# A four-layer graph network on one Trainium2 core: the list schedule gets other durations, a charge for TensorE's changes of mode, and a shorter period

## The chip, the cores and the metric

The kernel runs on one core of a Trainium2 chip. The core has five engines with instruction queues of their own: TensorE (PE in the profile, its weight loads PEld), VectorE (DVE), ScalarE (ACT), GpSimd (POOL) and SyncE (SP, which here issues DMAs only). Each engine takes its instructions in the order in which the program gives them. The metric is device time in microseconds for one launch; several runs are taken and their median is given. A profile is one further execution.

## The reference

The input x is 32 samples of 512 nodes by 256 features, in float32, and one adjacency matrix of 512 x 512 for all samples. Four layers follow each other, each with a layer norm and a ReLU ahead of it and an addition to x behind it:

```python
h = max(layernorm(x), 0); x = x + L0(h)   # 4 heads of 64: softmax(q k^T / 8, masked) v, then wo
h = max(layernorm(x), 0); x = x + L1(h)   # MLP 256->512, GAT without mask, MLP 512->256, GAT with mask
h = max(layernorm(x), 0); x = x + L2(h)   # GAT, 4 heads of 64, masked
h = max(layernorm(x), 0); x = x + L3(h)   # GAT, 8 heads of 32, masked, with a prior, then W_out
# a GAT's weights: softmax over j of leaky_relu(f1[i] + f2[j])
```

Samples are independent of each other; within a sample the layers are not.

## The kernel before, in words

After the weights and masks are prepared, `pipelined` (L493) builds the program of all 32 samples as a list of steps, and a planner puts the steps in order.

**What a step is.** `q = Plan(nc, PERIOD)` (L525) stands in for the engines. A call such as `q.vector.tensor_tensor(...)` is only recorded (`Plan.add`, L87): it becomes a `Step` with its engine, its duration from `cost` (L253), the tiles that it touches, and the earlier steps that it must follow. A step of TensorE inside `with q.unit(t):` joins several matmuls to one step of t microseconds, which are then issued together. All recorded calls are issued from L217, so that the profile has this one line for nearly everything and groups are told apart by the names of tiles.

**How the order comes about.** `Plan.order` (L116) simulates the engines. Each step has a tail, the longest chain of durations behind it in its sample, with `HOP` for each handover between steps, and a due time (L129), where `PERIOD` is 90:

```python
step.due = s * self.period - step.tail
```

Steps that take something out of a PSUM bank on another engine than TensorE get a due time 1000 earlier. Then, over and over, of all steps whose predecessors are planned and for which buffers are to be had, the one with the smallest pair (start, due) is taken (L113, L167 to L182); its start is the later of the time when its engine is free and the time when its inputs are ready. The clock of the engine goes on by the step's duration (L186). So due times decide between steps that could start at the same time, and start decides before due. At most `AHEAD` = 3 samples beyond the oldest unfinished one may take part (L171). Buffers are counted: 61 blocks of 128 x 512 in SBUF, 8 PSUM banks, 4 tiles x. The result is one order; each engine's queue is filled in that order (`issue`, L213), and on the chip semaphores hold an instruction until its inputs are there. The planner's durations don't slow anything on the chip; they only set the order.

**The work of a sample.** `norm_t` (L546): `bn_stats` and `bn_aggr` on VectorE, `rs` as a power on GpSimd, `h` on VectorE, transposes into `pt` on TensorE, and `hT` on ScalarE. Matrix products over 128 x 128 of weights are `feature_major`, `node_major`, `node_major2` and `weighted` (tiles `mm` and `av`); they and the transposes use the whole array of TensorE. Three kinds of units use a part of it at a time:

- `sc` in layer 0 (L651): two heads at once, each on 64 rows of the array. ScalarE then takes the exponential, and VectorE multiplies the mask in.
- Layer 0's `av` and `sm` (L658): four products of 64 columns, two at a time, and four sums of 32 columns at once. `f1p` of layer 1 (L683): four products of 32 columns at once.
- Layers 2 and 3, `separable` (L803): for one block of 128 keys, j, VectorE makes four tiles `p` (L837), and a unit (L841) multiplies them into `av` and `sm`, with 64 and 32 columns in layer 2 (duration 2.85) and 32 columns in layer 3 (duration 1.92). `R`, which `p` reads, comes over DRAM by DMA (`rd`).

`normalise` (L604) takes sums through DRAM, for a reciprocal on all partitions, with four to seven DMAs on SP.

Of the kernel before, what the change touches and what calls it, by code (L numbers as in the profile page):

```python
# [19 lines left out]
N = 512  # L20
# [16 lines left out]
SAFE_PRIOR = 20.0  # L37


PERIOD = 90.0  # L40
BLOCKS, KEEP = 61, 12
KEEP_BANKS = 0

# [1 line left out]
class Step:  # L45


    def __init__(self, engine, busy):
        self.engine, self.busy, self.calls = engine, busy, []
        self.touches, self.before, self.after = [], [], []  # L50


class Plan:
# [6 lines left out]


    ENGINES = dict(tensor="PE", vector="DVE", scalar="ACT", gpsimd="POOL", sync="SP")
    HOP, AHEAD = 0.12, 3

    def __init__(self, nc, period):
        self.nc, self.period = nc, period
# [13 lines left out]
        self.samples.append([])  # L80
        self.history = {}

    def unit(self, busy):

        return _Unit(self, busy)

    def add(self, attribute, engine, op, args, kw):  # L87
        steps = self.samples[-1]
# [27 lines left out]
    def order(self):  # L116

        owners, left = {}, {}
        for s, steps in enumerate(self.samples):
            for step in steps:  # L120
                step.sample = s
                step.waits = len(step.before)
                step.ready = 0.0
                for name in step.touches:
                    left[name] = left.get(name, 0) + 1
                    owners[name] = s
            for step in reversed(steps):
                step.tail = step.lasts + max((n.tail + self.HOP for n in step.after), default=0.0)
                step.due = s * self.period - step.tail  # L129

                if step.engine != "PE" and any(self.tile_tag[name] == "bank" for name in step.touches):
                    step.due -= 1000.0
        free = {tag: [0.0] * bufs for tag, (bufs, _) in self.tags.items()}
        held = {}
        to_come = [{} for _ in self.samples]
        for name, s in owners.items():
            tag = self.tile_tag[name]
            to_come[s][tag] = to_come[s].get(tag, 0) + 1
        live, at = set(), {e: 0.0 for e in self.ENGINES.values()}
        open_ = {e: [] for e in at}  # L140
        for steps in self.samples:
            for step in steps:
                if not step.waits:
                    open_[step.engine].append(step)
        result, count = [], sum(map(len, self.samples))
        oldest = 0

        def slots(step):

            when, taken = 0.0, {}  # L150
            for name in step.touches:
                if name in live:
                    continue
                tag = self.tile_tag[name]
                keep = self.tags[tag][1]
                reserve = 0
                for s in range(oldest, step.sample):
                    if to_come[s].get(tag, 0):
                        reserve += max(0, min(keep, to_come[s][tag] + held.get((s, tag), 0)) - held.get((s, tag), 0))
                n = taken.get(tag, 0)  # L160
                if len(free[tag]) - n <= reserve:
                    return None
                when = max(when, sorted(free[tag])[n])
                taken[tag] = n + 1
            return when

        while len(result) < count:  # L167
            best = None
            for engine, waiting in open_.items():
                for step in waiting:  # L170
                    if step.sample > oldest + self.AHEAD:  # L171
                        continue
                    start = max(at[engine], step.ready)
                    if best is not None and self.key(start, step) >= best[0]:
                        continue
                    when = slots(step)
                    if when is None:
                        continue
                    start = max(start, when)
                    if best is None or self.key(start, step) < best[0]:  # L180
                        best = self.key(start, step), start, step
            assert best is not None, "the buffers do not suffice"  # L182
            _, start, step = best
            step.start = start
            open_[step.engine].remove(step)
            at[step.engine] = start + step.busy  # L186
            end = start + step.lasts
            for name in step.touches:
                tag, s = self.tile_tag[name], step.sample
                if name not in live:  # L190
                    live.add(name)
                    free[tag].remove(min(free[tag]))
                    held[s, tag] = held.get((s, tag), 0) + 1
                    to_come[s][tag] -= 1
                left[name] -= 1
                if not left[name]:
                    live.discard(name)
                    held[s, tag] -= 1
                    free[tag].append(end + self.HOP)
            for n in step.after:  # L200
                n.waits -= 1
                n.ready = max(n.ready, start + step.busy if n.engine == step.engine == "PE" else end + self.HOP)
                if not n.waits:
                    open_[n.engine].append(n)
            result.append(step)
            while oldest < len(self.samples) and not any(to_come[oldest].values()) and not any(
                n for (s, _), n in held.items() if s == oldest
            ):
                oldest += 1
        self.makespan = max(at.values())  # L210
        return result
# [15 lines left out]


class _Unit:
    def __init__(self, plan, busy):  # L230
        self.plan, self.busy = plan, busy

    def __enter__(self):
        self.plan.joined = Step("PE", self.busy)

    def __exit__(self, *_):
        self.plan.joined = None
# [14 lines left out]

def cost(engine, op, args, kw, out):  # L253

    n = 1
    for _, k in out.ap[1:]:
        n *= k
    if engine == "PE":
        if op == "transpose":
            return 0.11, 0.2  # L260
        return max(0.22, n * 0.00168), 0.2
    if engine == "ACT":
        return 0.08 + 0.00093 * n, 0.09 + (0.19 if "accum_out" in kw else 0.0)
    if engine == "DVE":
        if op == "reciprocal":
            return 0.07 + 0.00625 * n, 0.09
        return 0.066 + 0.00105 * n + (0.06 if op == "scalar_tensor_tensor" and n == N else 0.0), 0.09
    if engine == "POOL":
        return (1.05 if n < 16 else 0.2 + 0.0015 * n), 0.1
    return 0.1, 3.5  # L270


# [1 line left out]
def gnn_stack_kernel(ctx: ExitStack, tc: tile.TileContext, a: dict, out: bass.AP):  # L274
# [99 lines left out]
    with tc.tile_pool(name="prep", bufs=2) as prep, tc.tile_pool(name="prep_psum", bufs=1, space=PSUM) as pp:  # L374
# [17 lines left out]
        src = a["L2_a"]  # L392
# [60 lines left out]
        rows = []  # L453
# [39 lines left out]
    def pipelined(stack):  # L493
# [31 lines left out]
        q = Plan(nc, PERIOD)  # L525
# [103 lines left out]
        def layer0(xt):  # L629
# [15 lines left out]
            for m in range(KD):  # L645
                av, sm = bank("av"), bank("sm")
                for jj in range(0, NT, 2):
                    p = {}
                    for j in (jj, jj + 1):
                        sc = [bank("sc"), bank("sc")]  # L650
                        with q.unit(0.96):  # L651
                            for s, r in enumerate(rows):
                                q.tensor.matmul(sc[s], kT[m][r, col(j)], qT[m][r, :], start=True, stop=True)
                        for s in range(2):
                            p[j, s] = b = block("p0")
                            q.scalar.activation(b, sc[s], AF.Exp)
                            q.vector.tensor_tensor(b, b, mask0T[:, j, :], op=ALU.mult)
                    with q.unit(2.75):  # L658
                        for j in (jj, jj + 1):
                            for s, r in enumerate(rows):  # L660
                                q.tensor.matmul(
                                    av[r, :], half(v, j)[:, m * P + s * 64 : m * P + s * 64 + 64], p[j, s],
                                    start=(j == 0), stop=(j == NT - 1),
                                )

                        for n, b in enumerate(p.values()):
                            q.tensor.matmul(
                                sm[n * 32 : n * 32 + 32, :], ones[:, :32], b, start=(jj == 0), stop=(jj == NT - 2)
                            )
                normalise(oT[m], av, sm, 2, 2)  # L670
# [5 lines left out]
        def first_gat(o1):  # L676
# [3 lines left out]

            part, sd = block("part"), small("sd", NT, 2)
            f1p = bank("f1p")
            with q.unit(1.0):  # L683
                for k in range(KH):
                    q.tensor.matmul(f1p[k * 32 : k * 32 + 32, :], fr1a[:, k, :], o1[k], start=True, stop=True)
            q.scalar.copy(part, f1p)
# [116 lines left out]
        def separable(xt, w, nh, mask, bars):  # L803
# [23 lines left out]
            for g in range(nh // 4):  # L827
# [5 lines left out]
                for j in range(NT):  # L833
# [4 lines left out]
                            p[s], R[s], e[:, j, nh + h : nh + h + 1], mask[:, j, :], op0=ALU.max, op1=ALU.mult  # L838
                        )
                    st = dict(start=(j == 0), stop=(j == NT - 1))  # L840
                    with q.unit(1.92 if per == 4 else 2.85):  # L841
                        for s in range(4):
                            h, r0 = 4 * g + s, s % per * f
                            q.tensor.matmul(avs[s // per][r0 : r0 + f, :], half(v, j)[:, h * f : (h + 1) * f], p[s], **st)
# [464 lines left out]
```

## Time and profile before

| | |
|---|---|
| median of 3 runs | 4729.1 us (4728.43 to 4732.22) |
| the profiled execution | 4727.03 us |
| its span, first to last instruction | 4725.2 us |
| instructions | 55,985 |
| TensorE busy, matmuls | 4491.1 us (95%) |
| VectorE, ScalarE, GpSimd busy | 3061.7, 1642.7, 611.8 us |
| first matmul of the samples, last store issued | 108.2 us, 4721.3 us |

Busy time is the time that an engine's instructions cover. A matmul's record is longer than the distance to the next one's start, since they are pipelined, and its end is modelled. A chain line such as "2062.11 1.00 PE av L217 x8" has a start, a length and a number of instructions of one group in the sequence that ended last. A line of a wait names the waiting group and the one whose result it waited for, then the time in total, the number of times and the longest.

### The profile page before, as it was taken

How to read it: one execution, taken by the hardware profiler on the slowest of the kernel's cores; microseconds unless marked ns; L12 is line 12 of the kernel's file. 1: busy time of each engine (PE TensorE's matmuls, PEld its weight loads, DVE VectorE, ACT ScalarE, POOL GpSimd, SP SyncE). 2: the span in 40 equal slices, each digit the busy share in tenths (PEclk: the TensorE clock that was granted, in tenths of full speed). 3: DMA queues.
4: the chain of work that ended last, by engine and by line, in shares of the span. 5: the costliest groups of instructions: out<-in, count | busy, mean ns of one | idle time of the engine just before them, and what ended most of it. 6: DMA issues, size and time to landing. Idle time of an engine off the chain costs nothing.

```text
span 4725.2 us, 55985 instructions
## 1 busy us (share of the span) xinstructions
PE 4491.1 (95%) x20146; PEld 2069.3 (44%) x20146; DVE 3061.7 (65%) x6772; ACT 1642.7 (35%) x3508; POOL 611.8 (13%) x648
## 2 busy tenths in 40 slices
PE   2999999999999999999999999999999999999986
PEld 1444444444444444444444444444444444444442
DVE  5357676665667665677657776567666675667664
ACT  1343333333333333333333333333333333333321
POOL 1011111011101111111011110111110111101110
PEclk9999999999999999999999999999999999999997
DMA  2001111101111111111111111111011111111111
GB/s 85 10 18 50 34 46 38 43 30 37 38 40 35 44 39 30 46 44 37 35 36 34 44 46 37 33 38 49 28 44 31 41 42 45 29 39 35 42 36 42
DMA packets 168209, 183.04 MB, mean 39 GB/s; under 512 B 64370, under 2 KB 99956, under 8 KB 167924
## 3 DMA queue, kind: packets, MB, share of 16 engines
q1 hardware_dynamic: 161972, 173.10, 12.1%
q10 hardware_dynamic: 5408, 4.20, 0.3%
q8 instruction: 161, 2.64, 0.2%
q0 software_dynamic: 544, 2.10, 0.1%
q14 instruction: 124, 1.02, 0.1%
HBM read 159.92 MB, written 19.40 MB: 38 GB/s over the span
## 4 chain that ended last, share of the span: by engine, by line
PE 82%; DVE 10%; POOL 2%; ACT 2%; DMA 2%; issue 1%; SPq 0%; POOLq 0%; DVEq 0%; ACTq 0%
PE mm L217 34%; PE av L217 26%; PE sm L217 10%; PE pt L217 6%; PE sc L217 4%; DVE stats L217 2%; DVE x L217 2%; POOL rs L217 1%; DVE p L217 1%; DVE h L217 1%; PE f1p L217 1%; POOL p L217 1%; DVE ue L217 1%; DVE yT L217 1%; ACT e L217 1%
## 5 line engine op out<-in xcount | busy, mean ns | idle before, releaser
L217 PE MATMUL av<-p,v 128*128 128x512 f32 (+1 forms) x2048 | 726.2, 603 | 0.1
L217 DVE SCALAR_TENSOR_TENSOR p<-R,e,mask3T 128x512 f32<-128x512 f32 x1024 | 690.8, 748 | 14.3 <-DMA R<-rd 13.9
L217 PE MATMUL av<-p,vs 128*32 128x512 f32 (+1 forms) x3072 | 555.8, 604 | 14.1 <-DVE p L217 13.4
L217 PE MATMUL mm<-W_fc,o 128*128 128x512 f32 x1024 | 484.7, 602 | 0.0
L217 POOL TENSOR_TENSOR rs<-ve,mhalf 128x4 f32<-128x4 f32 x128 | 172.6, 1351 | 2087.1 <-DVE ve L217 1654.7
L217 PE MATMUL sm<-p,w 128*32 128x512 f32 x3072 | 424.8, 597 | 0.0
L217 DVE TENSOR_TENSOR p<-p,mask0T 128x512 f32<-128x512 f32 x512 | 348.1, 717 | 103.6 <-ACT p L217 102.6
L217 DVE SCALAR_TENSOR_TENSOR p<-R,e,mask1T 128x512 f32<-128x512 f32 x512 | 346.6, 748 | 80.1 <-DMA R<-rd 79.8
L217 ACT ACTIVATE p<-sc 128x512 f32<-128x512 f32 x512 | 274.8, 601 | 349.5 <-PE sc L217 348.0
L217 PEld LDWEIGHTS av<-p,v 128*128 128x128 f32 (+1 forms) x2048 | 243.4, 163 | 319.1 <-issue 274.4
L217 PEld LDWEIGHTS av<-p,vs 128*32 128x32 f32 (+1 forms) x3072 | 125.0, 118 | 369.8 <-issue 207.2
L217 POOL TENSOR_SCALAR p<-p,r 128x512 f32<-128x512 f32 x128 | 140.8, 1110 | 1103.2 <-DVE r L217 736.5
L217 PE MATMUL sc<-qT,kT 64*128 64x512 f32 x1024 | 280.9, 634 | 1.1 <-ACT s L217 0.9
L217 PEld LDWEIGHTS mm<-W_fc,o 128*128 128x128 f32 x1024 | 179.9, 190 | 183.1 <-issue 173.6
L217 PE MATMUL mm<-w,hT 128*128 128x272 f32 (+1 forms) x1024 | 255.8, 396 | 2.2 <-ACT hT L217 1.5
L217 DVE TENSOR_SCALAR h<-x,mv,rs 128x256 f32<-128x256 f32 x512 | 215.8, 475 | 62.0 <-POOL rs L217 61.6
L217 PE MATMUL mm<-o,mlp_w 128*128 128x512 f32 x512 | 235.0, 600 | 8.7 <-DVE o L217 8.7
L217 PE MATMUL pt<-ident,h 128*128 128x128 f32 x1024 | 169.4, 291 | 75.2 <-DVE h L217 73.3
L217 ACT COPY v<-mm 128x512 f32<-128x512 f32 (+1 forms) x256 | 122.7, 479 | 332.9 <-PE mm L217 325.8
L217 PE MATMUL mm<-hT,mlp_w 128*128 128x512 f32 x512 | 237.0, 605 | 0.8 <-ACT hT L217 0.7
L217 PE MATMUL av<-pT,v 128*128 128x512 f32 x512 | 233.3, 594 | 2.1 <-ACT pT L217 2.1
L217 DVE TENSOR_TENSOR vs<-mm,w 128x256 f32<-128x256 f32 x256 | 105.2, 420 | 188.6 <-ACT w L217 185.0
(188 smaller groups left out, 6124.5 us busy)
## 6 DMA issues: line engine op xcount, KB each, us to landing
R<-rd SPq DMA_DIRECT2D x384, 256.0 KB
x<-in_x_dram SPq DMA_DIRECT2D x32, 512.0 KB
rc<-s SPq DMA_DIRECT2D x128, 128.0 KB
rc<-s SPq DMA_DIRECT2D x256, 64.0 KB
out_dram<-x SPq DMA_DIRECT2D x32, 512.0 KB
adj<-in_adj_dram POOLq DMA_DIRECT2D x2, 1024.0 KB, 7.1
s<-sums SPq DMA_DIRECT2D x128, 8.0 KB
few<-s SPq DMA_DIRECT2D x128, 8.0 KB
```

Of the source, the lines that this page charges most:

```text
L217: getattr(getattr(self.nc, attribute), op)(*args, **kw)
```

## The change

It touches the planner and its numbers, and no computation.

- `PERIOD` is 55 for 90, and `HOP` 0.05 for 0.12.
- A step has a mode. Steps of TensorE are "full" unless a unit says otherwise: "rows" for `sc`, "columns" for the other units. When the planner compares steps of TensorE, one of another mode than the last planned one starts no earlier than `SWITCH` of that last mode after the engine is free.
- `cost` has other figures for most operations. For `bn_stats` and `reduce_max` it counts the elements of the input and no longer those of the output.
- The units have shorter durations. A unit covers one block of keys in `separable` as before.

```diff
-PERIOD = 90.0
+PERIOD = 55.0
@@ class Step
-    def __init__(self, engine, busy):
-        self.engine, self.busy, self.calls = engine, busy, []
+    def __init__(self, engine, busy, mode="full"):
+        self.engine, self.busy, self.mode, self.calls = engine, busy, mode, []
@@ class Plan
-    HOP, AHEAD = 0.12, 3
+    HOP, AHEAD = 0.05, 3
+    SWITCH = dict(full=0.094, columns=0.12, rows=0.2)
@@ Plan.order
-        result, count = [], sum(map(len, self.samples))
+        result, count, mode = [], sum(map(len, self.samples)), "full"
...
                     start = max(at[engine], step.ready)
+                    if engine == "PE" and step.mode != mode:
+                        start = max(start, at[engine] + self.SWITCH[mode])
...
             at[step.engine] = start + step.busy
+            if step.engine == "PE":
+                mode = step.mode
@@ class _Unit
-        self.plan, self.busy = plan, busy
+        self.plan, self.step = plan, Step("PE", busy, mode)
     def __enter__(self):
-        self.plan.joined = Step("PE", self.busy)
+        self.plan.joined = self.step
@@ def cost
+    src = args[1] if op in ("bn_stats", "reduce_max") else out
     n = 1
-    for _, k in out.ap[1:]:
+    for _, k in src.ap[1:]:
         n *= k
     if engine == "PE":
         if op == "transpose":
-            return 0.11, 0.2
-        return max(0.22, n * 0.00168), 0.2
+            return 0.109, 0.165
+        return max(0.2, n * 0.001676), 0.165
     if engine == "ACT":
-        return 0.08 + 0.00093 * n, 0.09 + (0.19 if "accum_out" in kw else 0.0)
+        return 0.08 + 0.00095 * n, 0.085 + (0.19 if "accum_out" in kw else 0.0)
     if engine == "DVE":
         if op == "reciprocal":
-            return 0.07 + 0.00625 * n, 0.09
-        return 0.066 + 0.00105 * n + (0.06 if op == "scalar_tensor_tensor" and n == N else 0.0), 0.09
+            return 0.07 + 0.00625 * n, 0.085
+        return 0.066 + 0.00105 * n + (0.06 if op == "scalar_tensor_tensor" and n == N else 0.0), 0.085
     if engine == "POOL":
-        return (1.05 if n < 16 else 0.2 + 0.0015 * n), 0.1
+        return (1.3 if n < 16 else 0.15 + 0.0016 * n), 0.1
@@ units
-                        with q.unit(0.96):
+                        with q.unit("rows", 0.86):
-                    with q.unit(2.75):
+                    with q.unit("columns", 2.63):
-            with q.unit(1.0):
+            with q.unit("columns", 0.86):
-                    with q.unit(1.92 if per == 4 else 2.85):
+                    with q.unit("columns", 1.72 if per == 4 else 2.6):
```

More of the change, by code (lines that the diff above doesn't have):

```diff
@@ L81, in begin, with unit @@
         self.history = {}
-    def unit(self, busy):
-        return _Unit(self, busy)
+    def unit(self, mode, busy):
+        return _Unit(self, mode, busy)
     def add(self, attribute, engine, op, args, kw):
@@ L229, with __init__ @@
 class _Unit:
-    def __init__(self, plan, busy):
-        self.plan, self.busy = plan, busy
+    def __init__(self, plan, mode, busy):
+        self.plan, self.step = plan, Step("PE", busy, mode)
     def __enter__(self):
-        self.plan.joined = Step("PE", self.busy)
+        self.plan.joined = self.step
     def __exit__(self, *_):
```

## The prediction

> **What bounds the kernel now.** I read the page first (busy shares, slices, the chain's shares), then the stretches, then TensorE's waits, then the chain piece by piece.
>
> ```profile
> span 4725.2 us, 55985 instructions
> PE 4491.1 (95%) x20146; PEld 2069.3 (44%) x20146; DVE 3061.7 (65%) x6772; ACT 1642.7 (35%) x3508; POOL 611.8 (13%) x648
> ...
> PEclk9999999999999999999999999999999999999997
> ...
> PE 82%; DVE 10%; POOL 2%; ACT 2%; DMA 2%; issue 1%; SPq 0%; POOLq 0%; DVEq 0%; ACTq 0%
> ```
>
> TensorE is 95% busy and carries 82% of the chain that ended last. The next engine, VectorE, is at 65%. The question is what TensorE's busy time contains. Busy time of three stretches (columns: us, then PE, PEld, DVE, ACT, POOL with instruction counts, granted clock, DMA share, GB/s):
>
> ```profile
> 2100.00:2667.00 567.00, 555.42 (x2509) 255.28 (x2508) 375.85 (x829) 202.55 (x437) 76.61 (x80) 0.99 0.13 39
> 4467.00:4610.00 143.00, 125.02 (x540) 61.40 (x541) 87.92 (x197) 44.45 (x100) 19.15 (x19) 0.94 0.12 36
> 4610.00:4721.00 111.00, 70.11 (x301) 32.49 (x299) 55.55 (x113) 13.85 (x38) 5.47 (x6) 0.78 0.13 39
> ```
>
> The first is the steady state: loads of x are issued at 2108.1, 2675.3 and 3241.1 us, every fourth sample, so the order repeats each 567 us, 4 samples, 141.7 us a sample. The last is the drain: the last three stores are issued at 4487.0, 4610.6 and 4721.3 us, and in the last 111 us TensorE is idle for 41 and gets 0.78 of its clock. Who TensorE waited for in the steady period (us in total, times, longest):
>
> ```profile
> PE pt L217 <- DVE h L217: 5.3, 5, 2.1
> PE mm L217 <- ACT hT L217: 2.5, 1, 2.5
> PE mm L217 <- DVE o L217: 1.4, 1, 1.4
> PE pt L217 <- POOL p L217: 1.4, 2, 1.3
> ```
>
> 7.8 of 11.1 us of named waits belong to one chain, norm_t: stats, rs on GpSimd, h, transposes, hT. Then the chain that ended last, in order of time (start us, us, what):
>
> ```profile
> 2062.11 1.00 PE av L217 x8
> 2063.11 0.86 PE sm L217 x8
> 2063.97 0.86 PE av L217 x8
> 2064.83 0.86 PE sm L217 x8
> 2065.68 1.06 PE mm L217 x4
> 2066.74 1.00 PE av L217 x8
> 2067.74 0.86 PE sm L217 x8
> 2068.60 1.06 PE sc L217 x4
> ```
>
> Eight column-tiled matmuls take 0.86 us after their own kind and 1.00 after another; an untiled or a row-tiled group takes 1.06 where 0.86 is its length. A change of mode costs 0.14 to 0.20 us and counts as busy.
>
> **What the Trainium skill says.** "TensorEngine Tiling (Array Packing)", Key Properties: "Changing tiling mode (not just tile) drains the TensorE". The lines above agree and price it. "Perfetto Trace Analysis", Tensor Engine Instruction: matmul ends are computed, not observed, so I work with starts. "TensorE: Matmul & The Clock Gate", Part 1: idle stretches give the clock back; the 0.78 in the drain agrees. No page prices a planner's order.
>
> **The accounting of a steady period.** I take the distance between matmul starts (0.43 us for 512 columns, two passes a call, so 0.86 a call; 0.216 a pass for 256; 0.109 a transpose; four 32-column or two 64-column tiles together 0.43). Times their counts this is 521 us in 567. Mode changes over 16 samples (1533 to 3800 us), at the switch and in the first matmuls after it: untiled to columns 124 x 0.13 = 16.1; columns to untiled 128 x 0.21 = 26.9; untiled to rows 76 x 0.20 = 15.2; back 72 x 0.20 = 14.4; rows to or from columns 76 x 0.17 = 12.9; between 64 and 32 columns 180 x 0.136 = 24.5. Sum 110, so 6.9 us a sample, 27.4 a period. The rest, 567 - 521 - 27.4 = 18.6 us a period, is waiting: 11.1 named above, and short stalls. So 8% of the steady time is not work.
>
> **The change, part by part.** No instruction is added or removed; 55,985 remain. What moves is the order, on every engine's queue and SP's and POOL's too.
>
> 1. *Mode changes in the plan (SWITCH, mode of a unit).* Another mode's step now starts 0.094 to 0.2 us later in the planner's eyes than one of the current mode, and start is compared before due: TensorE stays in a mode until nothing of it is ready. Now 200 untiled runs stand in 16 samples, median 3.6 us, and 164 column runs, median 2.9: mostly one unit. VectorE makes the four p of a unit in 4 x 0.663 = 2.65 us (pitch of the p rows), while column work takes 616 us of these 2267, so units pile up while untiled work runs, and runs grow. The four untiled edges cost 72.6 us per 16 samples, 4.5 a sample. Bounds: half of the runs gone saves 2.3 a sample, 73 us in all; none gone, 0. I take a third: 1.5 x 32 = **48 us**. The 24.5 us inside units (64 to 32 columns both carry the mode "columns") stays.
>
> 2. *Durations.* Against the trace: bn_stats was planned at 0.072 us, has a pitch of 0.326, and is now 0.335. Four a norm: the plan was 1.0 us short. rs was 1.05, is 1.351 in the mean (19 of 128 over 2 us), now 1.3: 0.3 short. HOP was 0.12; from an end to the waiting start I measure 0.032 to 0.055 between TensorE, ScalarE and VectorE; now 0.05. Over some six hops this error ran the other way, 0.4 us. Net, norm_t was planned 0.9 us too short, 2.1 with a slow rs, and TensorE waits in just that place. Units: rows 0.96 to 0.86, columns 2.75, 2.85 and 1.92 to 2.63, 2.6 and 1.72, with the change now charged apart: measured 0.86, 2.58 + 0.12 inside, 1.72. All better. Steps of TensorE that would wait are now planned later, with other samples' work ahead of them. What covers it is that work of up to four samples; if it is not ready the wait stays. Late next would be GpSimd's p (planned 0.97, measured 0.69 to 1.6) and the DMAs (3.5 planned). Bounds: from nothing to all but 4 us of the 18.6 a period. I take half, 9.3 x 7.2 periods (400 to 4470 us) = **67 us**.
>
> 3. *PERIOD 90 to 55.* The due time of the next sample comes 35 us earlier. x still has four buffers and AHEAD is 3, so no more samples run at once; the newest catches up faster. In the drain the last sample stands alone for 35 us less, of 111 us with 41 idle: 35 x 41/111 = 13, with the slower clock **15 us**. Bounds 0 and 45. In the steady state it costs nothing while TensorE has ready work of other samples; if samples in one phase compete for the 8 banks and 61 blocks, it costs what rival C says.
>
> DMAs move with their steps. SP issues in order; the period shows it waiting 189.3 us for rT and 183.8 for raw, so a store planned early holds R behind it, and p waits for R (10.9 us a period on VectorE). VectorE is idle 191 us in 567, which covers that. GpSimd, at 13%, has room.
>
> Sum: 48 + 67 + 15 = 130 us. Against the profiled execution, 4727.0 us (span 4725.2 and 1.8 around it), 4597; that run lies 2.1 us under the median 4729.1, so 4599. I say **4600 us**.
>
> **Rivals.**
> - *A, nearly all waits go and half of the runs.* 14.6 x 7.2 = 105, with 73 and 30: 4520 us. For it: the norm chain holds most named waits and is just what is refitted. Against: slow rs and DMA landings stay unplanned. The floor, 130.3 a sample x 32 + 108 before the first matmul of the samples + 49 inside units, 4327, is not the limit.
> - *B, the waits move.* A step planned later to spare one wait makes another late: only parts 1 and 3 remain, 63 us, 4666 us. For it: TensorE is 98% busy in the period by the page, so named waits are few and scattered.
> - *C, slower: modes lock out urgent steps.* A row-tiled sc or a column unit with an early due now waits for the end of an untiled run, up to 35 us already. Its p blocks fill up, VectorE stops, and when the run ends TensorE uses four p in 1.72 us where VectorE makes them in 2.65. The gain of B is used up when this adds 63/32 = 2 us of waiting a sample; at 3.5 us a sample the time is 4729 - 63 + 112 = 4778 us. Against: VectorE's slack of 48 us a sample.
> - *D, the order hardly differs*, within 0.2% (9.5 us), about what a measurement here can tell from no change. Against: every PE duration and the compared start change.
>
> **How the numbers follow.** Forecast 0.52 (4545 to 4655), A 0.12 (4440 to 4545), B 0.22 (4655 to 4719), C 0.11, D 0.03. Faster 0.86, same 0.03, slower 0.11. The range 4515 to 4710 leaves out C, D, the lower part of A and the edge of B, some 2 in 10.
>
> **What would show it.** Part 1: fewer and longer runs, column groups of 0.86 us following each other in the chain, and 130 to 140 untiled runs in 16 samples for 200. Part 2: h and hT leave the top of TensorE's waits, and a steady sample takes about 138 us or less for 141.7. Part 3: the last two stores stand nearer than 111 us. The forecast is wrong if the period's waits stay at 18 us under other names (B), or TensorE's share falls below 95% with p, o or oT ahead of it (C).

## The result, and the profile after

The changed kernel takes 4505.4 us (median of 4 runs, 4502.08 to 4508.63), the kernel before 4729.1. The ratio is 0.9526, with a 95% interval of 0.9509 to 0.9542: 4.7% faster, 224 us. The forecast was 4600 with a range of 4515 to 4710. The direction was right and the gain much too small: 129 us forecast, 224 measured, 10 us below the range.

The page of the kernel after:

```profile
span 4506.8 us, 55379 instructions
PE 4351.9 (97%) x20146; PEld 2125.3 (47%) x20146; DVE 3017.6 (67%) x6772; ACT 1613.0 (36%) x3508; POOL 547.0 (12%) x648
...
PE 91%; DVE 5%; DMA 2%; issue 1%; ACT 1%; POOL 1%; SPq 0%; ACTq 0%; POOLq 0%; DVEq 0%
```

The same 20,146 matmuls, with the same work, cover 139 us less: part of what had counted as busy was not work. The busy share rose to 97% and the chain's share on TensorE from 82% to 91%. (606 instructions of the sequencers went with the new order; the engines' own counts are the same. The prediction had said that all 55,985 would remain.)

Stretches, with the columns as before: four samples of the steady state (stores at 2080.3 and 2614.4 us, 133.5 us a sample for 141.7), and the two parts of the drain.

```profile
2083.20:2617.30 534.10, 533.10 (x2510) 261.52 (x2509) 368.66 (x829) 198.50 (x436) 67.28 (x80) 1.00 0.13 41
4218.00:4427.00 209.00, 188.63 (x826) 95.97 (x826) 142.12 (x308) 63.18 (x148) 23.84 (x29) 0.93 0.13 42
4427.00:4503.00 76.00, 50.23 (x246) 21.42 (x242) 42.18 (x84) 8.05 (x22) 1.04 (x1) 0.82 0.13 43
```

TensorE is idle for 1.0 us in 534, where it had been idle for 11.6 in 567. All its named waits in those four samples are one line; it replaces the 11.1 us of before, and the transposes that waited for h are gone from it:

```profile
PE mm L223 <- ACT hT L223: 1.0, 4, 0.2
```

The chain in order of time, inside one sample of the steady state:

```profile
2157.66 0.99 PE av L223 x8
2158.66 0.86 PE sm L223 x8
2159.52 0.86 PE av L223 x8
2160.38 0.86 PE sm L223 x8
2161.23 0.86 PE av L223 x8
2162.09 0.86 PE sm L223 x8
...
2172.39 1.03 PE pt L223 x8
2173.42 7.07 PE sc L223 x32
2180.49 3.31 PE mm L223 x14
2185.39 1.87 PE av L223 x8
2187.26 1.00 PE sm L223 x8
2188.25 1.87 PE av L223 x8
2190.12 1.00 PE sm L223 x8
```

All eight units of layer 3 stand in one row, and only the first column group pays 0.99; all eight sc units stand together (x32, 0.88 us each, where one alone took 1.06). Before, groups of 1.00 and 1.06 alternated. The last eight units, of layers 0 and 2, still pay inside: 1.87 and 1.00 for 1.72 and 0.86, a change between 64 and 32 columns each time.

**The accounts.** I took the prediction's accounting to the whole of both traces: the distance between starts, less the length of the work, split into changes of mode (at the switch and in the matmuls just after it) and waiting, which is all the rest. The line between the two is drawn by a rule, so that single figures may shift by a few us between them; their sum doesn't. "Steady" is from the sixth store to the 29th, 23 samples; ramp and drain lie around it.

| | before | after | difference |
|---|---|---|---|
| changes among untiled, rows, columns | 939 | 238 | -701 |
| time of all changes, those inside units too | 219.6 us | 109.9 us | -110 |
| waiting, steady | 116.7 us | 16.3 us | -100 |
| waiting, drain | 92.2 us | 80.1 us | -12 |
| waiting, ramp | 30.6 us | 35.9 us | +5 |

The sum, -217, answers to the 218.4 us between the two profiled executions (4727.0 and 4508.6).

Not all of the 116.7 us is time in which TensorE stood still. In the steady state of the trace before, nine stretches of 3.4 us have half the clock; after, there is none. One of them, in the trace before (the stretch, whose third number from the end is the granted clock, then two of TensorE's instructions, with the wait ahead of the first in brackets):

```profile
2202.90:2206.30 3.40, 2.79 (x4) 1.24 (x5) 3.40 (x12) 3.40 (x10) 1.08 (x2) 0.50 0.11 24
```

```profile
2203.51 2.07 PE L217 MATMUL mm<-hT,wqT 128*128 128x512 f32 x2 [2.49 <-ACT hT L217]
2205.38 1.50 PE L217 MATMUL mm<-hT,wkT 128*128 128x512 f32 x2
```

After a wait of 2.49 us the first pair of matmuls takes 1.87 us from start to start, where a pair takes 0.86. Each of the nine stretches begins within 3.4 us of the start of a wait of 1.7 to 2.5 us. From the starts I estimate some 14 us of such slow work in them. So a wait of TensorE could cost more here than its own length, and that part went with the waits.

### The profile page after: what moved, and what is told of

It is laid out like the page before. It is cut to its first block, busy times and chain, and to the rows that moved or that the text cites. A ratio compares the mean times of both kernels' runs of the same rounds, so it can differ in the third digit from the quotient of the medians.

```text
span 4506.8 us, 55379 instructions
## 1 busy us (share of the span) xinstructions
PE 4351.9 (97%) x20146; PEld 2125.3 (47%) x20146; DVE 3017.6 (67%) x6772; ACT 1613.0 (36%) x3508; POOL 547.0 (12%) x648
## 3 DMA queue, kind: packets, MB, share of 16 engines
q1 hardware_dynamic: 161972, 173.10, 12.6%
## 4 chain that ended last, share of the span: by engine, by line
PE 91%; DVE 5%; DMA 2%; issue 1%; ACT 1%; POOL 1%; SPq 0%; ACTq 0%; POOLq 0%; DVEq 0%
PE mm L223 39%; PE av L223 28%; PE sm L223 10%; PE pt L223 6%; PE sc L223 5%; DVE p L223 2%; PE f1p L223 1%; ACT hT L223 0%; DVE stats L223 0%; DMA x<-in_x_dram 0%; DVE x L223 0%; POOL rs L223 0%; PE fb L223 0%; DVE h L223 0%; DMA beta<-in_beta_dram 0%
## 5 line engine op out<-in xcount | busy, mean ns | idle before, releaser
L223 DVE SCALAR_TENSOR_TENSOR p<-R,e,mask3T 128x512 f32<-128x512 f32 x1024 | 711.0, 755 | 9.8 <-DMA R<-rd 9.5
L223 PE MATMUL av<-p,v 128*64 128x512 f32 (+1 forms) x2048 | 713.2, 601 | 1.4 <-DVE p L223 1.4
L223 DVE TENSOR_TENSOR p<-p,mask0T 128x512 f32<-128x512 f32 x512 | 321.7, 679 | 388.7 <-ACT p L223 388.6
L223 POOL TENSOR_TENSOR rs<-ve,mhalf 128x4 f32<-128x4 f32 x128 | 137.6, 1075 | 2949.9 <-DVE ve L223 2681.7
L223 PE MATMUL mm<-W_fc,o 128*128 128x512 f32 x1024 | 457.5, 592 | 0.0
L223 PEld LDWEIGHTS av<-p,v 128*64 128x64 f32 (+1 forms) x2048 | 249.4, 163 | 352.0 <-issue 282.8
L223 ACT COPY sums<-sm 128x512 f32<-128x512 f32 x128 | 75.0, 586 | 798.6 <-PE sm L223 736.6
L223 PE MATMUL mm<-w,hT 128*128 128x272 f32 (+1 forms) x1024 | 276.5, 398 | 2.7 <-ACT hT L223 2.6
L223 PE MATMUL sc<-qT,kT 64*128 64x512 f32 x1024 | 231.9, 598 | 0.3 <-ACT hT L223 0.3
L223 PEld LDWEIGHTS mm<-w,hT 128*128 128x128 f32 x1024 | 185.2, 193 | 61.8 <-ACT p L223 18.9
```

Source lines behind the costliest of these rows:

```text
L223: getattr(getattr(self.nc, attribute), op)(*args, **kw)
```

## The experiments

The change has three parts that can be set alone: the charge for a change of mode, the durations (cost, HOP and units' lengths together), and the period. Diffs are against the changed kernel unless said otherwise. Ratios are to the kernel before in the same runs.

**One part taken back.** e1 leaves the charge out:

```diff
-                    if engine == "PE" and step.mode != mode:
-                        start = max(start, at[engine] + self.SWITCH[mode])
```

> The changed kernel without the charge for a change of mode (new durations and period 55 stay). The order then has 1182 changes among untiled, rows and columns for 238. Theory S (switches and waits are separate accounts: the charge removes switches, the durations remove waits): 944 changes more at about 0.165 us are 156 us, waits stay near 0.7 us a sample, so 4660 us. Theory G (the charge does both: long runs let other modes' work pile up, and so the waits go too): waits come back to 4 us a sample as well, 4750 us or more. Theory D (the durations do nearly all): 4560 us or less.

Measured: 4719.0 us, ratio 0.9974 (0.9964 to 0.9984). Nearly the whole gain is gone. The trace has the 1182 changes, 252.8 us for 109.9, and waits of 83.5 us in the steady state for 16.3. So neither the sum of separate accounts (4660) nor the durations alone give it: it lies between S and G, nearer to G. The chain of e1, in order of time, has two column units and then untiled work again, where eight units stood in a row after the change:

```profile
2119.96 4.29 PE mm L221 x10
2124.25 1.87 PE av L221 x8
2126.12 0.99 PE sm L221 x8
2127.11 1.87 PE av L221 x8
2128.98 0.99 PE sm L221 x8
2129.97 2.77 PE mm L221 x6
```

e2 puts the old durations back:

```diff
-    HOP, AHEAD = 0.05, 3
+    HOP, AHEAD = 0.12, 3
...
-        return max(0.2, n * 0.001676), 0.165
+        return max(0.22, n * 0.00168), 0.2
...
-                        with q.unit("rows", 0.86):
+                        with q.unit("rows", 0.96):
...
```

> The changed kernel with the old durations (cost, HOP and units as before; charge and period 55 stay). The order has 233 changes of mode for 238. Theory S: switches stay at 3.4 us a sample, the waits come back by about 100 us: 4610 us. Theory G: the waits stay away, 4500 to 4530 us. Theory D: 4690 us.

Measured: 4555.9 us, ratio 0.9629 (0.9613 to 0.9645). Changes cost 105.5 us, as after, and steady waits 77.0 us. The durations are worth 50 us here, half of what S expected.

e3 puts the period back:

```diff
-PERIOD = 55.0
+PERIOD = 90.0
```

> The changed kernel with period 90. The order has 365 changes of mode for 238. If the period works on the drain alone, as predicted: 15 us of drain and 127 x 0.165 = 21 us of switches, 4540 us. If the steady state needs the closer samples as well (waits of 1 us a sample more or other): 4570 us or more. If it does nothing: 4505 us.

Measured: 4614.1 us, ratio 0.9752 (0.9736 to 0.9768), slower than every expectation but the open-ended one. Of the 109 us (105 between the profiled executions), 21 are changes (131.3 us), 56 steady waits (72.5), 20 waits in the drain (99.9) and 8 in the ramp (43.5). In this order the steady state lost something that the one of 55 had.

**One part alone.** e4 is the kernel before with the new durations, that is, the changed kernel with e1's edit and e3's:

```diff
-PERIOD = 55.0
+PERIOD = 90.0
...
-                    if engine == "PE" and step.mode != mode:
-                        start = max(start, at[engine] + self.SWITCH[mode])
```

> The kernel before with the new durations alone (no charge, period 90). The order has 1032 changes of mode for 939 of before. Theory S: the waits go, 100 us, the switches grow by 93 x 0.165 = 15 us: 4645 us. Theory G: the waits stay, 4730 us or slower. Theory D: 4530 us.

Measured: 4631.5 us, ratio 0.979 (0.9773 to 0.9806). Steady waits fall from 116.7 to 39.9 us, changes rise from 219.6 to 232.0. This is S's reading, within 14 us.

e5 is the charge alone, that is, e2's edit and e3's:

```diff
-PERIOD = 55.0
+PERIOD = 90.0
-    HOP, AHEAD = 0.05, 3
+    HOP, AHEAD = 0.12, 3
...
```

> The kernel before with the charge for a change of mode alone (old durations, period 90). The order has 280 changes of mode for 939. If the charge works by the switches alone: 659 x 0.165 = 109 us less, 4622 us, with waits as before. If longer runs take the steady waits along, as e2 (183.8 us of waiting and drain for 239.5) hints: 4560 us. If long runs lock urgent steps out without the new durations and period: over 4660 us.

Measured: 4661.8 us, ratio 0.9858 (0.9842 to 0.9875). Changes fall to 115.8 us, nearly as much as in the whole change, but steady waits rise from 116.7 to 141.0 us. Its transposes wait longest (waits of TensorE from 1500 to 3500 us; the last two lines are those of the kernel before in the same stretch):

```profile
PE pt L223 <- DVE h L223: 16.4, 17, 2.2
PE pt L223 <- POOL p L223: 11.8, 9, 3.4
```

```profile
PE pt L217 <- DVE h L217: 18.5, 18, 2.1
PE pt L217 <- POOL p L217: 4.3, 6, 1.3
```

The wait for h was there before and did not grow; the wait for p did, from 4.3 to 11.8 us. The growth of the waits, 24 us, could be the prediction's rival C, urgent steps held back by a long run; that this is its cause is not shown. It is much smaller than what the charge saves, 104 us of changes.

e6 is the period alone, against the kernel before:

```diff
-PERIOD = 90.0
+PERIOD = 55.0
```

> The kernel before with period 55 alone. The order has 1244 changes of mode for 939: 305 x 0.165 = 50 us more, and with the drain 12 us shorter 4770 us. If closer samples are good in themselves, as the prediction took them: 4715 us. If they help only where modes are charged, as e1 beside e4 hints (88 us slower with 55 than with 90 when nothing is charged): 4770 to 4820 us.

Measured: 4714.6 us, ratio 0.9965 (0.9953 to 0.9978). The 4715 us that closer samples should give are met, but not in the way meant: changes cost 35 us more (254.7) and steady waits 42 us less (74.5).

All eight combinations, in us (before: 4729.1 to 4732.0 over all runs):

| | period 90 | period 55 |
|---|---|---|
| nothing else | 4729.1 | 4714.6 |
| durations | 4631.5 | 4719.0 |
| charge | 4661.8 | 4555.9 |
| charge and durations | 4614.1 | 4505.4 |

The period is worth 15 us, -88, 106 or 109, the charge 67, 17, 159 or 214, and the durations 98, -4, 48 or 50, by what stands beside them. That is no sum of parts, and each of the eight is only one order: the next runs show that a meaningless step of a number can move the time by 70 us.

One effect is the same in all four pairs: the charge lowers the number of changes (939 to 280, 1032 to 365, 1244 to 233, 1182 to 238) and their time by 101 to 149 us. On the steady waits it has no such constant effect: they rise by 24, 33 and 2.5 us in three pairs and fall by 67 in the fourth, from e1 to the changed kernel. The durations lower them by 61 to 77 us in three pairs and raise them by 9 in the fourth, e6 to e1.

**What is the period?** e7 sets 50, e9 sets 55.1 and e10 sets 47, and nothing else:

```diff
-PERIOD = 55.0
+PERIOD = 50.0
```

> The changed kernel with period 50 for 55. The order has 391 changes of mode for 238. If nearness of samples is what period 55 brings, 50 is as good or better but for the switches, 153 x 0.165 = 25 us: 4500 to 4535 us. If 55 stands for one order that happens to be good, and a small step of the period gives another one altogether: 4560 to 4600 us.

> The changed kernel with period 55.1 for 55. Nothing that the period is for changes by a tenth of a microsecond, but ties between due times fall otherwise, and the order has 382 changes of mode for 238. Theory O (what 55 brings is one order among many, and the number only picks it): 144 x 0.165 = 24 us of switches, and waits as with period 50, 4560 to 4595 us. If the gain is a property of the period's size: 4505 us, at most 4530 with the switches.

> The changed kernel with period 47. The order has 236 changes of mode for 238, and orders of the periods 43 to 48 all have 234 to 240. Theory O with the switches as the sign of a good order: as many switches, so within 20 us of the changed kernel, 4485 to 4520 us, though 50 lies between and gave 4593. If nearness past 55 costs something in itself (50 slower than 55 for that reason): 4600 us or more.

Measured: 4592.7 us (ratio 0.9708, 0.9692 to 0.9724), 4575.9 us (0.9673, 0.9657 to 0.9689) and 4497.8 us (0.9508, 0.9493 to 0.9524). A tenth of a microsecond of period costs 70 us; a step of 5 costs 87 and one of 8 gains 8. So between 47 and 55.1 it is not the size of the period that decides: it picks one of many orders. The trace of e9 has 382 changes (135.2 us) and steady waits of 44.5 us. Its waits of TensorE in the same stretch of 1500 to 3500 us are short:

```profile
PE mm L223 <- ACT hT L223: 3.8, 15, 0.3
```

So most of the 44.5 us are stalls that the view of waits doesn't name, which is why I count from the starts.

**Do truer durations take waits away, or do they too only pick an order?** e11, e13 and e14 hold old durations (e2's edit) at the periods 50, 52 and 60, and e15 the new ones at 43, against the others, all with the charge:

> The changed kernel with the old durations and period 50, to be held beside e7 (new durations, period 50, 4592.7 us, 391 changes of mode). This order has 226 changes. If truer durations are what takes the waits away: slower than e7 or like it, 4590 to 4640 us. If the kind of order decides, and with it the durations only by which order they lead to: 165 x 0.165 = 27 us of switches less and the waits of e2, so 4540 to 4570 us, faster than with the truer durations.

> The changed kernel with the old durations and period 52; 223 changes of mode. If truer durations remove waits among orders that are equally good in switches: waits in the steady state as in e2 and e11 (65 to 77 us), 4545 to 4565 us. If e2 and e11 were accidents of their orders: anything from 4490 us on.

> The changed kernel with the old durations and period 60; 199 changes of mode, the fewest of all orders with the old durations. If truer durations remove waits: 5 us of switches less than e2, else as e2, 4540 to 4565 us, not under 4530. If the number of switches alone makes the time: 4500 us.

> The changed kernel with period 43; new durations, 239 changes of mode. If truer durations remove waits: 16 to 20 us of waits in the steady state, 4490 to 4510 us. If not: 4540 us or more is as likely.

| durations, period | us | ratio, interval | changes of mode | steady waits, us |
|---|---|---|---|---|
| old, 50 (e11) | 4551.7 | 0.9621 (0.9605 to 0.9637) | 226 | 65.1 |
| old, 52 (e13) | 4580.9 | 0.9681 (0.9665 to 0.9697) | 223 | 92.0 |
| old, 55 (e2) | 4555.9 | 0.9629 | 233 | 77.0 |
| old, 60 (e14) | 4545.7 | 0.9605 (0.9589 to 0.9621) | 199 | 66.8 |
| new, 43 (e15) | 4494.0 | 0.9499 (0.9483 to 0.9515) | 239 | 33.0 |
| new, 47 (e10) | 4497.8 | 0.9508 | 236 | 20.2 |
| new, 55 (after) | 4505.4 | 0.9526 | 238 | 16.3 |
| new, 50 (e7) | 4592.7 | 0.9708 | 391 | 69.6 |

At period 50 the old durations are 41 us faster than the new ones, since the new ones fall on an order with 391 changes. Among orders with 199 to 239 changes the old ones stand between 4546 and 4581 us with 65 to 92 us of steady waits, the new ones between 4494 and 4505 with 16 to 33. The two sets, four orders and three, don't overlap. So both are true: the durations are worth some 40 to 87 us in orders that are equally good in changes, and a number in the planner may lose that again by the order it falls on. e13 missed the range that truer durations would give by 16 us on the slow side; e15 was met but with 33 us of waits for the 16 to 20 expected.

**A change of tile width, priced.** e8 turns every second unit of layers 0 and 2, so that its sums come ahead of its products (`sums3` holds the four matmuls into `sm` that stood behind them; layer 0 is edited in the same way):

```diff
...
+                        if j % 2:
+                            sums3()
                         for s in range(4):
                             h, r0 = 4 * g + s, s % per * f
                             q.tensor.matmul(avs[s // per][r0 : r0 + f, :], half(v, j)[:, h * f : (h + 1) * f], p[s], **st)
...
+                        if not j % 2:
+                            sums3()
```

> The changed kernel with every second unit of layers 0 and 2 turned: sums (32 columns) first and products (64 columns) after them, so that neighbouring units meet in the same tile width. The order of steps is the same; changes of tile shape on TensorE fall from 710 to 559. At 0.145 us each, as measured inside column runs, 22 us less: 4483 us. If a change between 64 and 32 columns costs nothing once the array is in columns: 4505 us.

Measured: 4484.4 us, ratio 0.948 (0.9464 to 0.9495), 21.0 us less than the changed kernel for 151 changes less: 0.139 us each, beside 0.145 expected. The waiting, counted from the starts, is the same within 1 us. The chain shows neighbouring units meeting in one width:

```profile
2183.19 1.87 PE av L223 x8
2185.05 1.00 PE sm L223 x8
2186.05 3.58 PE av L223 x16
2189.63 1.85 PE sm L223 x16
2191.49 3.58 PE av L223 x16
2195.07 1.85 PE sm L223 x16
```

Two units take 3.58 + 1.85 = 5.43 us, where they took 2 x (1.87 + 1.00) = 5.74.

**A version that beats both.** e12 has the turned units of e8, period 47 and the prices of the trace:

```diff
-    SWITCH = dict(full=0.094, columns=0.12, rows=0.2)
+    SWITCH = dict(full=0.14, columns=0.21, rows=0.2)
-PERIOD = 55.0
+PERIOD = 47.0
```

> A version meant to beat both: period 47, every second unit of layers 0 and 2 turned as in e8, and the charge at the prices that the trace of before showed (0.14 from untiled, 0.21 from columns, 0.2 from rows). The order has 182 changes of mode for 238, and 532 changes of tile shape for 559 in e8. From e8 (4484 us): 27 x 0.16 = 4 us less, and if period 47 is as good as 55: 4480 us. If the higher charge holds urgent steps back: over 4500 us.

Measured: 4470.0 us, ratio 0.9448 (0.9432 to 0.9464): 35 us faster than the changed kernel and 10 us faster than expected, with 182 changes, 82.0 us for all changes and 20.3 us of steady waits, as in e10 (20.2). Alone, the turned units gave 21 us (e8) and period 47 gave 8 (e10); the higher charge was not run alone, but a sign that it held steps back is missing.

## Why the prediction was wrong, point by point

**What bounds the kernel, and the accounting: right.** TensorE stayed the bound, and the two accounts outside its work, changes and waits, are where the gain came from. The split of a steady sample into work, 6.9 us of changes and the rest proved good: the same account of the trace after closes to within 2 us of the measured difference.

**Part 1, "I take a third": the first term that was mis-sized, 48 us for 110.** A run is a stretch of TensorE in one mode. Untiled runs fell from 12.6 to 3.1 a sample in 16 steady samples (49 runs, where I had named 130 to 140). Even my upper bound, half the runs and 73 us, was too low. I had let units pile up while untiled work ran, and taken the run lengths of before for granted. But by the planner's code the rule ends a run only when nothing of its mode can start within the charge, so a longer run of one mode lets more work of the next pile up. That the charge makes the long runs is shown by the pairs above; this account of why they came out so long is argued from the code. In each steady sample there are now two column runs for 17 units and one run of rows for eight. The prices held but for one: 0.14 for a change inside columns was confirmed by e8, while from columns to untiled it is 0.14 in the steady state after, where a transpose comes next each time, for 0.21 before. "TensorEngine Tiling (Array Packing)", Key Properties, of the Trainium skill, says that a change of mode drains the engine; the gap of 0.09 to 0.11 us at each switch agrees. I had left the changes inside units as they were; they grew from 49 to 67 us, as units now follow each other. So the changes between modes, which the 48 stood for, fell by about 128 us, and 18 of these were lost again inside the units.

**Part 2, "I take half": the second, 67 us for 100 in the steady state.** The place was right: in the steady stretch 54 us of 117 stood at the transposes of h before, and 10 of 16 after. Half was too little: the durations alone (e4) took 77 us away. What I did not see is how much depends on the order that they lead to. With old durations and the charge, steady waits are 65 to 141 us (e2, e5, e11, e13, e14); with new durations and no charge, 40 (e4) or 84 (e1); with both, 16 to 33 in the good orders and 45 to 73 in the others (e3, e7, e9). And of the 18.6 us a period that I took for waiting, some were matmuls at half the clock, by the estimate above 14 of 117 us in the whole steady state.

A rival was at hand in the prediction, the slow rs, which no duration covers: over 2 us in 19 of 128 before, in 3 after. But it doesn't carry the waits. With old durations (e2, e11, e13, e14) none of the 128 is slow, and 65 to 92 us of waits stay; with new ones alone (e4) 12 are slow, and 40 us stay.

**Part 3, the drain: right in size, in part by luck, and wrong in what it stood for.** Waits in the drain fell by 12 us for 15, and the last two stores are 75.4 us apart for 110.7. But the period alone (e6) took only some 3 us of waits out of the drain; beside the charge and the durations (e3) it is 20. And I wrote that the period costs nothing in the steady state, and judged it by its size. e3 and e9 show that it works through the order: taken back to 90 it costs 109 us, of which 20 lie in the drain; moved by 0.1 it costs 70.

**The rivals.** A (4520 us, 0.12) was the nearest and still 15 us short: nearly all waits went, as it said, but it too let only half of the runs go. B, that waits move, is excluded by the 16.3 us of steady waits, named or not, for 116.7. C may be behind the 24 us more of waits in e5, and does not decide. D is excluded by 701 changes fewer. The error was not in naming the outcome but in its chance: I took middle values of both terms as if they were independent, while the eight runs show that what one part is worth depends on the others.

**What stays open.** Why the charge and the period gain so much more together (the table of eight), or whether that is more than the luck of these orders, was not settled. In the trace of after each steady sample repeats the one before; with period 90 and the charge (e3, e5) the stores come at uneven distances for half the run or all of it. A repeating order can't be all that makes the waits vanish: with the old durations and period 60 (e14) the stores are 135.8 us apart throughout the steady state, and 66.8 us of waits stay.

## What to carry to other kernels

When TensorE is 98% busy, look for what its busy time hides: count the changes of tile mode and multiply by their price, taken from the starts of matmuls. In a list schedule, size a rule that prefers to stay in a mode by the runs that are left at the end (here a few a sample), not by a share of those of before. And before a planner's number is credited with a gain, move it by a meaningless amount: here 0.1 us moved the time by 70 us, and several orders have to be compared before a reading such as "truer durations are worth 50 us" stands.

## What the runs showed of the hardware that was not expected

- A change of mode costs more than the gap at the switch, and what follows has a part in it. In the trace of before that gap was 0.094 to 0.114 us; the matmuls just after it lost another 0.02 to 0.10, so that untiled to columns came to 0.13, columns to untiled to 0.21, and to or from rows up to 0.22. From columns to a matmul of 256 columns or more it was 0.22 us in the median, to a transpose of h 0.17 (traces of e1 and after).
- A change between 64-column and 32-column tiles costs the same kind of price, 0.139 us by taking 151 of them out (e8), though both tile the columns.
- Eight row-tiled units in one run took 7.07 us, 0.88 each; one alone took 1.06.
- The same rs on GpSimd took 1.04 us in the median before and over 2 us in 19 of 128 cases, in e1 in 29 and in e2 in none. The step just ahead of it on GpSimd doesn't settle this: right after a step on e it took 2.5 us in the median before (13 cases) and 1.02 after (27 cases). Why is open.
- The half clock follows short waits, but not each of them: in the steady state before, nine of the 17 waits of 1.69 us or more were followed by 3.4 us at 0.50 of the clock, and none of the 12 waits of 1.25 to 1.45 us.
